# In the last image, q, k and the MLP's first layer use the two PSUM banks of the scan's gates

## The chip, the cores and the metric

The kernel runs on one core of one Trainium2 chip. The core has five instruction streams that run side by side and meet at semaphores: PE (matrix multiply; the profile shows its weight loads apart, as PEld), DVE (vector), ACT (scalar activation functions), POOL (general vector work) and SP, which here issues DMA transfers. Matmul results land in PSUM, which the program cuts into eight tiles of 128 partitions by 512 fp32 numbers; such a tile is called a bank below. The metric is the device time of one execution, in microseconds (us).

## The reference

Two layers work on a batch of 8 images of 192 channels by 64x64 pixels, in fp32.

Layer 0 widens to 384 channels with a 1x1 convolution, applies a 3x3 depthwise convolution, and forms gates from a 16-channel projection. In four directions it scans each chunk of eight columns:

```python
hn = l * x + gl * h_up + gm * h + gr * h_dn      # gl, gm, gr normalized by |gl| + |gm| + |gr| + eps
```

The four scans are weighted and added, normalized over channels, scaled by a global response norm (which needs sums over the whole image), and projected back to 192 channels.

Layer 1 is window attention on 8x8 windows with six heads, and an MLP:

```python
shortcut = _layer_norm(xs, norm1_g, norm1_b)
qkv = (xin @ qkv_w.T + qkv_b)                                     # 64 tokens per window
attn = einsum(_l2n(q), _l2n(k)) * temperature
attn = where(attn >= 16th largest of the row, attn, -100)
out = softmax(attn + rpb) @ v  ->  proj
x2 = shortcut + out
hdn = gelu(_layer_norm(x2) @ fc1_w.T + fc1_b) @ fc2_w.T + fc2_b   # 192 -> 768 -> 192
return x2 + hdn
```

## The kernel before

The kernel handles one image as three generators of steps: `front` (widening and convolution), `scan` (the gated scan, which ends in a per-image scale `sc`, `bb`), and `windows`, which runs `window_row` for each of the eight rows of windows. A row of windows is 8 image lines, 512 tokens, four tiles of 128 tokens. The front of image b+1, the scan of image b and the window rows of image b-1 are written down side by side. The window rows of the last image (b = 7) need the whole scan of that image, and no other scan follows; they run alone at the end.

Inside `window_row` the steps are, by line: load `zg` (L1032) and scale it (L1037); project tokens in two steps (L1052) with the first layer norm (L1059 to L1085); transpose the result into `sT` (L1017, L1025); project q and k, one step per tile of 128 tokens, each with its own PSUM tile `pq` (L1097, L1102), which ACT reads twice, once to copy it to `qk` (L1110) and once to square it (L1118); project the values (L1141, L1153); normalize q and k (L1162 to L1176) and transpose them (L1189, L1197); scores (L1217, L1231); top 16, mask, softmax (L1244 to L1298); transpose the attention (L1312, L1320); attend (L1332, L1345); project and add (L1366, L1378); second layer norm (L1389 to L1421); transpose to `xT` (L1434 to L1441); the MLP's first layer in three steps, each of which writes a pair of PSUM tiles `ph` (L1448, L1453, L1457) that ACT evacuates with the bias (L1464); GELU over all 768 hidden channels (L1473), then the activation table is set back (L1474); second layer plus residual (L1487), evacuation (L1501) and store.

PSUM is split into two pools. `n_ps` has two tiles under the tag `nb`; only `tile_of` of the scan uses it, for one of its gates (L678, `nb`). `l_ps` has six tiles under the tag `lp`; everything that calls `bank()` shares them, all the scan's other matmuls and all of `window_row`. One row of windows takes 34 tiles from it: 2 for tokens, 2 for `sT`, 4 `pq`, 2 for values, 4 to transpose q and k, 3 scores, 3 to transpose the attention, 2 to attend, 2 projections, 2 for `xT`, 6 `ph`, 2 for the second layer.

Nothing is issued while the generators run. `Held` is a tile that will be made later, and each `plan(engine, cost, fn, r=, w=)` records a step with what it reads and writes. `Plan.order` then schedules all steps of all eight images: a list scheduler that keeps a clock for every engine, models how long each step holds its engine (`act(n)`, `mm(slots, n)`, `dma(n)` = 350 ns of issue per transfer plus 2600 to landing, GELU 5400) and gives a step its PSUM tile only when one of its tag is free in the model. A step that makes two tiles starts when both are free. Within one tag and one `plan.lane`, steps that make tiles start in the order in which they were written; `window_row` changes the lane from stage to stage (`sT`, q, k and values are lane 7, the MLP lane 10), and the scan (lane 0) is kept a tile when it is ready for one. Among steps that can start without delay, the lowest `rank` goes first. `order` makes twelve rounds (`RUNS`): the first with ranks from the place in the program, each later one with due times from the round before, and keeps the round whose modelled length is shortest. The steps are then issued in that order on every engine. Each engine works through its stream in order, so a step that waits holds up all behind it on that engine.

The buffers in SBUF that set the distance between rows are `zg`, `qk`, `at`, `x2`, `xn` and `hd` with one copy, and `s0` and `v` with two.

Of the kernel before, what the change touches and what calls it, by code (L numbers as in the profile page):

```python
# [31 lines left out]
P = 128  # L32
B, DM, H, W = 8, 192, 64, 64
# [255 lines left out]
def tile_ss2d_then_window_attention(ctx: ExitStack, tc: tile.TileContext, a: dict, out: bass.AP):  # L289
# [164 lines left out]
    n_ps = ctx.enter_context(tc.tile_pool(name="n_ps", bufs=2, space=PSUM))  # L454
# [13 lines left out]
    log_c = {}  # L468
    log_half = blank("log_half", [P, 1], math.log(0.5) / 3)

    def bank(name="lp"):
        return Held(l_ps, [P, 512], name, tag="lp")

    def rsqrt(v, key, shape, name, gain=1.0):
# [20 lines left out]
    def front(b, xs, xsT):  # L495
# [14 lines left out]
        def project(ct, s):  # L510

            own = padded[ct * P : (ct + 1) * P]
            cols = slice(ct * P, (ct + 1) * P)
            pins = [bank() for _ in range(2)]

            def products():
# [27 lines left out]
        def convolve(ct, s):  # L544

            own = padded[ct * P : (ct + 1) * P]
            pc = bank()
            for k in range(2):
                strip = strips[k]
# [63 lines left out]
    def scan(b, xs, xsT, z, made):  # L613
# [14 lines left out]
        def proxy(t):  # L628

            x0 = Held(spool, [P, CT, 512], "x0", bufs=1)  # L630
            plan("SP", dma(), lambda: nc.sync.dma_start(x0(), xs()[:, :, t, :]), r=[xs], w=[x0])
            px = bank()

            def products():
# [374 lines left out]
    def window_row(b, g, z, sc, bb):  # L1009
# [84 lines left out]
        qk = Held(lpool, [P, NT, DIN], "qk", bufs=1)  # L1094
        nn = Held(small, [P, NT, 12], "nn")
        for tt in range(NT):
            pq = bank()  # L1097

            def projected(tt=tt, pq=pq):
                tok = slice(tt * P, (tt + 1) * P)  # L1100
                for ci in range(2):
                    nc.tensor.matmul(  # L1102
                        pq()[:, 0:DIN], lhsT=sT[:, ci, tok], rhs=w_qk[:, ci, :], start=ci == 0, stop=ci == 1
                    )

            plan("PE", mm(2, DIN), projected, r=["sT"], w=[pq, (qk, "room")])
            plan(
                "ACT",
                act(DIN),
                lambda tt=tt, pq=pq: nc.scalar.copy(qk()[:, tt, :], pq()[:, 0:DIN]),  # L1110
                r=[pq],
                w=[(qk, tt)],
            )
            sq = Held(lpool, [P, DIN], "sq", bufs=1)
            plan(
                "ACT",
                act(DIN),
                lambda pq=pq, sq=sq: nc.scalar.activation(sq(), pq()[:, 0:DIN], AF.Square),  # L1118
                r=[pq],
                w=[sq],  # L1120
            )
            plan(
                "DVE",
                vec(DIN),
                lambda tt=tt, sq=sq: nc.vector.tensor_reduce(
                    nn()[:, tt, :], sq().rearrange("p (h d) -> p h d", d=HD), AX.X, ALU.add
                ),
                r=[sq],
                w=[(nn, tt)],
            )  # L1130
            yield
# [313 lines left out]

        hd = Held(lpool, [P, NM, GT], "hd", bufs=1)
        for m2 in range(NM // 2):
            ph = [bank() for _ in range(2)]  # L1448

            def widened(m2=m2, ph=ph):  # L1450
                for k in range(2):
                    cols = slice((2 * m2 + k) * P, (2 * m2 + k + 1) * P)
                    nc.tensor.matmul(ph[k](), lhsT=w_f1[:, 0, cols], rhs=xT[:, 0, :], start=True, stop=False)  # L1453
                for k in range(2):
                    cols = slice((2 * m2 + k) * P, (2 * m2 + k + 1) * P)
                    own = slice(64 * k, 64 * k + 64)
                    nc.tensor.matmul(ph[k](), lhsT=w_f1[own, 1, cols], rhs=xT[own, 1, :], start=False, stop=True)  # L1457

            plan("PE", mm(3, GT), widened, r=["xT"], w=ph + [(hd, "room")])
            for k in range(2):  # L1460
                plan(
                    "ACT",
                    act(600),
                    lambda m=2 * m2 + k, p=ph[k]: nc.scalar.activation(  # L1464
                        hd()[:, m, :], p(), AF.Identity, bias=b_f1[:, m : m + 1]
                    ),
                    r=[ph[k]],
                    w=[(hd, 2 * m2 + k)],
                )
            yield  # L1470
# [51 lines left out]
    def windows(b, z, made):  # L1522
        for g in range(NG):
            yield from window_row(b, g, z, *made[b])
# [107 lines left out]
```

## Time and profile before

| what | us |
|---|---|
| median of 3 runs | 8295.51 (8274.17 to 8303.1) |
| the profiled execution's own time | 8293.82 |
| its span, first to last instruction | 8292.0 |
| PE / DVE / ACT / POOL busy in the span | 6951.0 / 6381.9 / 5488.0 / 5859.7 |
| last closing square of the last scan on ACT (L933) | 7782 |
| busy from 7860 to 8240: PE / ACT / DVE / POOL | 315.24 / 311.23 / 195.40 / 71.88 |

The span is the stretch that the trace covers; the profiled execution took 1.8 us more. A busy share is an average over stages: over the whole span the four engines are all between 66% and 84%, while after 7790 us DVE and POOL are mostly idle. "Idle before, releaser" names what ended an engine's wait. In the chain each step is followed back to what released it, so a wait that stands there delayed the end of the kernel. A matmul of fp32 numbers appears as two matmul instructions in the counts.

### The profile page before, as it was taken

The page shows a single profiled execution, that of the slowest core. Times are in us where ns is not written, and L with a number is a line of the kernel's source. Part 1 is how long each engine was busy: PE and PEld are TensorE (multiplying, and loading weights), DVE is VectorE, ACT ScalarE, POOL GpSimd, SP SyncE. Part 2 cuts the span into 40 slices and gives each one's busy share as a digit, 9 for nine tenths or more (in the row PEclk, how much of TensorE's full clock was granted, in tenths as well). Part 3 has the DMA queues.
Part 4 walks back from the last instruction along what each step waited for, and adds up shares of the span by engine and source line. Part 5 has one row for each costly group of instructions (what it writes and reads, how often), then busy time and mean ns, then how long its engine had stood idle before and what let it go on. Part 6 is the DMA issues. An engine that isn't in the chain of part 4 may idle for free.

```text
span 8292.0 us, 147108 instructions
## 1 busy us (share of the span) xinstructions
PE 6951.0 (84%) x51224; PEld 3600.7 (43%) x51224; DVE 6381.9 (77%) x15421; ACT 5488.0 (66%) x12537; POOL 5859.7 (71%) x5918
## 2 busy tenths in 40 slices
PE   5677688788988898888988898888888789888887
PEld 2333344444444444444444444444444444444454
DVE  1366777888788987888788887888888888888643
ACT  1355346766677666777577766777677676677787
POOL 0377877788778877788778777778788788877411
PEclk8887579788898788888898889888788887778898
DMA  6776146111542135411532126311111112111110
GB/s 175 193 191 180 42 128 165 50 44 45 139 129 74 52 96 138 107 45 56 157 103 77 46 76 171 91 46 46 57 41 50 43 41 66 41 48 41 30 22 15
DMA packets 1037948, 695.70 MB, mean 84 GB/s; under 512 B 704115, under 2 KB 860214, under 8 KB 1037206
## 3 DMA queue, kind: packets, MB, share of 16 engines
q1 hardware_dynamic: 1035830, 684.99, 30.9%
q8 instruction: 407, 6.67, 0.3%
q14 instruction: 335, 2.74, 0.1%
q10 hardware_dynamic: 1376, 1.30, 0.1%
HBM read 453.43 MB, written 232.67 MB: 83 GB/s over the span
## 4 chain that ended last, share of the span: by engine, by line
PE 23%; ACT 15%; DVE 14%; POOL 9%; DMA 5%; issue 4%; SPq 0%; POOLq 0%; DVEq 0%; ACTq 0%
PE g L678 6%; PE lp L1487 3%; PE lp L1453 2%; ACT at L1286 2%; ACT at L1298 2%; DMA zg<-z 2%; POOL pr L796 2%; PE lp L1052 2%; PE lp L565 2%; DVE pr L742 1%; PE lp L1102 1%; POOL pr L781 1%; ACT ab L735 1%; DMA strip<-pad 1%; POOL ab L766 1%
## 5 line engine op out<-in xcount | busy, mean ns | idle before, releaser
L678 PE MATMUL g<-xe,w_g 32*128 32x512 f32 x3648 | 1281.3, 777 | 284.0 <-DVE dx L833 90.3
L678 PE MATMUL g<-xo,w_g 32*128 32x512 f32 x3648 | 1218.2, 767 | 270.1 <-DVE dx L833 154.0
L796 POOL TENSOR_TENSOR pr<-pr,rr 128x512 f32<-128x512 f32 x672 | 872.5, 1298 | 369.4 <-ACT rr L779 320.5
L781 POOL TENSOR_TENSOR pr<-pr 128x512 f32<-128x512 f32 x672 | 887.2, 1321 | 339.7 <-DVE pr L742 254.8
L766 POOL TENSOR_TENSOR ab<-ab 128x512 f32<-128x512 f32 x672 | 873.4, 1300 | 269.6 <-ACT ab L735 264.7
L735 ACT ACTIVATE ab<-g 128x512 f32<-128x512 f32 x1344 | 778.7, 594 | 295.1 <-PE nb L678 175.5
L847 POOL TENSOR_TENSOR dx<-dx,hu 128x512 f32<-128x512 f32 x576 | 738.8, 1294 | 257.6 <-DVE hu L838 250.8
L565 PE MATMUL lp<-strip,w_cv 128*32 128x256 f32 x9216 | 678.3, 438 | 289.0 <-DMA strip<-pad 265.9
L785 POOL TENSOR_TENSOR pr<-pr 128x512 f32<-128x512 f32 x672 | 884.2, 1316 | 20.6
L678 PEld LDWEIGHTS g<-xe,w_g 32*128 32x128 f32 x3648 | 451.9, 219 | 835.0 <-DVE dx L833 206.5
L678 PEld LDWEIGHTS g<-xo,w_g 32*128 32x128 f32 x3648 | 423.4, 217 | 812.4 <-DVE dx L833 278.4
L777 ACT ACTIVATE rr<-nb,eps 128x512 f32<-128x512 f32 x672 | 460.4, 685 | 436.5 <-DVE nb L774 320.8
L1487 PE MATMUL lp<-hd,w_f 128*64 128x256 f32 (+1 forms) x2304 | 610.1, 505 | 63.4 <-ACT hd L1473 39.7
L792 DVE SCALAR_TENSOR_TENSOR nb<-nb,rr 128x512 f32<-128x512 f32 x672 | 464.7, 692 | 237.6 <-ACT rr L779 236.1
L565 PEld LDWEIGHTS lp<-strip,w_cv 128*32 128x32 f32 x9216 | 313.5, 122 | 659.3 <-issue 388.6
L855 POOL TENSOR_TENSOR y<-y,dx 128x512 f32<-128x512 f32 x384 | 593.9, 1555 | 1.8
L800 DVE SCALAR_TENSOR_TENSOR nb<-nb,pr 128x512 f32<-128x512 f32 x672 | 464.4, 691 | 152.5 <-POOL pr L796 148.1
L774 DVE TENSOR_TENSOR nb<-nb,ab 128x512 f32<-128x512 f32 x672 | 464.7, 691 | 128.9 <-POOL ab L766 98.8
L845 POOL TENSOR_TENSOR y<-hu,dx 128x512 f32<-128x512 f32 x192 | 247.3, 1296 | 418.8 <-DVE hu L838 415.7
L757 ACT ACTIVATE nb<-nb 128x512 f32<-128x512 f32 x672 | 397.8, 592 | 206.5 <-DVE pr L742 107.8
L838 DVE TENSOR_TENSOR hu<-g,hid 128x512 f32<-128x512 f32 x768 | 511.4, 678 | 4.6 <-PE g L678 1.7
L678 PE MATMUL nb<-xe,w_g 32*128 32x512 f32 x672 | 506.4, 844 | 8.8 <-DVE hid L807 8.6
(202 smaller groups left out, 17104.4 us busy)
## 6 DMA issues: line engine op xcount, KB each, us to landing
strip<-pad SPq DMA_DIRECT2D x1152, 132.0 KB
xd<-xsT SPq DMA_DIRECT2D x384, 256.0 KB
pad<-xin SPq DMA_DIRECT2D x192, 264.0 KB
xs<-st SPq DMA_DIRECT2D x192, 256.0 KB
xsT<-sn SPq DMA_DIRECT2D x192, 256.0 KB
xd<-xs SPq DMA_DIRECT2D x192, 256.0 KB
x<-xs SPq DMA_DIRECT2D x64, 768.0 KB
z<-y SPq DMA_DIRECT2D x64, 768.0 KB
```

The lines of the kernel that those rows point to most:

```text
L565: nc.tensor.matmul(pc()[q * RG : (q + 1) * RG, k * 256 : (k + 1) * 256].rearrange("p (h w) -> p h w", h=4), lhsT=w_cv[:, ct, q, dx, :], rh ...
L678: nc.tensor.matmul(dst, lhsT=w[rows, col : col + P], rhs=xp[rows, :], start=True, stop=True)
L735: lambda r=r: nc.scalar.activation(ab()[:, r, :], g[r](), AF.Abs),
L766: plan("POOL", gp(512), lambda: nc.gpsimd.tensor_add(ab()[:, 0, :], ab()[:, 0, :], ab()[:, 1, :]), w=[ab])
L774: plan("DVE", vec(512), lambda: nc.vector.tensor_add(nb(), nb(), ab()[:, 0, :]), r=[ab], w=[nb])
L781: plan("POOL", gp(512), lambda: nc.gpsimd.tensor_add(one(), one(), pr()[:, 1, :]), r=[(pr, 1)], w=[(pr, 0)])
L785: lambda: nc.gpsimd.tensor_add(one(), one(), pr()[:, 2, :]),
L796: plan("POOL", gp(512), lambda: nc.gpsimd.tensor_mul(one(), one(), rr()), r=[rr], w=[(pr, 0)])
L838: lambda: nc.vector.tensor_mul(like(hu(), d), like(pu(), d), state(d, ct)),
L847: plan("POOL", gp(512), lambda: nc.gpsimd.tensor_add(dx(), dx(), hu()), r=[hu], w=[dx])
L855: nc.gpsimd.tensor_add(y, y, dx().rearrange("p (c i) -> p i c", c=CH))
L1487: nc.tensor.matmul(dst[:, at : at + rhs.shape[-1]], lhsT=lhsT, rhs=rhs, **flags)
```

## The change

`bank` gets an argument `last`. With it, the tile comes from `n_ps` under the tag `nb` and not from `l_ps`. Two places pass it, and only for the last image: the four `pq` of each row and the three pairs `ph`. In the other seven images nothing is written differently. Matmuls, evacuations, costs and lanes are the same. In the last image ten of a row's 34 tiles come from the two `nb` tiles, and 24 from the six `lp` tiles. The planner sees the tags, so the order that it writes can differ too.

```diff
-    def bank(name="lp"):
+    def bank(name="lp", last=False):
+        if last:
+            return Held(n_ps, [P, 512], "nb")
         return Held(l_ps, [P, 512], name, tag="lp")
...
         for tt in range(NT):
-            pq = bank()
+            pq = bank(last=b == B - 1)
...
         for m2 in range(NM // 2):
-            ph = [bank() for _ in range(2)]
+            ph = [bank(last=b == B - 1) for _ in range(2)]
```

## The prediction

> **What bounds the kernel now.** The page comes first. Its engine line says that no engine is full over the span; its slices say where to look, because the change names the last image alone.
>
> ```profile
> PE 6951.0 (84%) x51224; PEld 3600.7 (43%) x51224; DVE 6381.9 (77%) x15421; ACT 5488.0 (66%) x12537; POOL 5859.7 (71%) x5918
> ...
> PE   5677688788988898888988898888888789888887
> ...
> DVE  1366777888788987888788887888888888888643
> ...
> POOL 0377877788778877788778777778788788877411
> ```
>
> DVE and POOL fall away in the last two to three slices of 207 us: the scan is over there and only window rows run. The last scan's closing square on ACT stands at 7782 us in the chain, so the stretch that the change can touch directly is the 510 us from there to 8292. The table by windows gives its steady part and its drain:
>
> ```profile
> 7860.00:8240.00 380.00, 315.24 (x2915) 199.62 (x2905) 195.40 (x981) 311.23 (x870) 71.88 (x201) 0.90 0.08 18
> ...
> 8240.00:8292.00 52.00, 35.49 (x260) 19.78 (x258) 2.93 (x10) 21.19 (x37) 1.94 (x10) 0.88 0.06 16
> ```
>
> The columns after the length are busy PE, PEld, DVE, ACT and POOL, then the clock and DMA. PE is busy 315 of 380 us and ACT 311, so PE and ACT bound the tail together: 65 us of PE idle time is all that any better order could win there. The scores of successive rows start at 7950.5, 8004.9, 8057.7 and 8107.2 us, about 52 us apart. The list of PE's waits in the same stretch says what ends that idle time:
>
> ```profile
> PE lp L1487 <- ACT hd L1473: 19.0, 3, 6.8
> ...
> PE lp L1312 <- ACT ot L1501: 4.6, 2, 2.3
> ...
> PE lp L1312 <- ACT qk L1110: 2.1, 3, 0.7
> ```
>
> The last two are waits for a bank: L1312 transposes `at`, and neither L1501 nor L1110 writes `at`; each frees a bank. They are 6.7 us together. The large one is data: the second layer waits for GELU.
>
> The chain, through one row, shows whose delay reaches the next row:
>
> ```profile
> 8015.97 0.02 issue
> 8016.00 2.22 ACT zg L1037 x3
> 8018.22 0.09 ACT ss_q L485
> 8018.31 1.15 ACT hd L1464 x2
> ...
> 8020.65 3.22 PE lp L1453 x4
> 8023.87 1.11 PE lp L1457 x4
> 8024.98 1.25 ACT hd L1464 x2
> ...
> 8028.01 2.76 ACT hd L1473
> ```
>
> The third pair of the MLP's first layer (L1453, L1457), its evacuation (L1464) and GELU (L1473) lie on it; GELU and evacuation are there in all eight rows of the last image.
>
> **How the banks are used now.** From the timelines of PE, ACT and DVE I took, for every PSUM tile from 7860 to 8240 us, its life from the first matmul that writes it to the end of its last reader. All six banks are taken at once for 32 us of the 380. The tiles that the change moves are alive for 335 bank-us (q, k: 28 tiles at 12.0) and 269 (first layer: 42 tiles at 6.4), 604 in all, and for 116 us there are three or more of them. After the change they have two banks, 760 bank-us: 79% used if no life gets shorter. The rest, 583 bank-us, has six banks, 2280: 26%. So the change relieves a pool that is full 8% of the time, and squeezes the tiles that held three banks or more 31% of the time.
>
> **The change part by part.** No instruction is added or removed and no DMA; the same matmuls, evacuations and stores run on the same engines. What changes is which bank a tile waits for, and through the planner the order on each queue (on SP that of the `zg` loads and the stores, on POOL that of the small norms; neither gets more to do). The sum is against the profiled execution, 8293.8 us (span 8292.0 and 1.8 around it), which stands 1.7 us under the median of 8295.5.
>
> First layer. Each of the three steps of a row takes two banks at once and writes both. Now the next pair finds other banks free: pairs start at 8261.51, 8264.95 and 8267.92, back to back. With two banks, pair n+1 can start only when both evacuations of pair n are done. Starting from the end of the first pair's evacuation as the profile has it, two more pairs follow, each 3.05 us of PE, 1.30 of evacuation and 0.10 of hand-over: 8.9 us to the end of the third evacuation. Row by row, first evacuation's end plus 8.9 against the third's end now: 7914.4 and 7919.8 give +3.5; 7965.1 and 7970.0, +4.0; 8019.5 and 8026.2, +2.2; 8073.1 and 8077.8, +4.2; 8121.8 and 8126.7, +4.0; 8171.1 and 8176.8, +3.2; 8223.2 and 8227.9, +4.2; 8266.3 and 8272.3, +2.9. That is 28.2 us by which GELU starts later over eight rows. The last two rows have next to nothing else to run, so their 7.1 count in full. In the other six (21.1) ACT has eight to sixteen exponentials (1.9 to 3.9 us) behind GELU that a new order can put ahead of it, which covers part; but the pair also waits where ACT itself stands in front of the `zg` transfer (2.63 us at 8016.0), since L1464 is queued behind L1037. I take three quarters, 15.8. Sum 22.9; bounds 2.9 (the last row alone) and 28.2. What is queued on PE behind a waiting pair is the next row's transposes (L1017) and its q and k (L1102); on ACT, behind the late evacuation, GELU and the shares.
>
> q and k. In four rows (7920, 8026, 8078, 8177 us) all four projections, 4.78 us of PE, run while ACT is in GELU, so that the second layer then starts without idle time; their banks are freed only 10.3 us after the matmuls, on average. With two banks, two projections (2.4 us) lose that place. The nearest cover is the two value projections (3.0 us), which read the same `sT` and keep their place among six banks. If it is used, the cost is nothing: the late pair takes the values' old place. If it is not, PE idles 2.4 us per row; and the second layer's first half, 5.31 us at 8031.4 where PE came without a gap, took 7.71 at 8233.9 after 6.82 idle, another 2.4. Bounds 0 and 19.2 (4.8 x 4). I take 2.4 x 4 = 9.6: the first pair's squares and copies (4 x 0.47 = 1.9) must also be pulled ahead of exponentials that are on the chain.
>
> Relief. The 6.7 us of L1312's bank waits can go; the ceiling is the 32 us in which six banks were taken. I take 6.7, because those are the waits that PE showed. What is late next there is `at` itself: at 8044.4 the transposes of the third part need the shares that end at 8043.2, so one of those waits shrinks to about half, and I don't count more.
>
> Sum: 8293.8 + 22.9 + 9.6 - 6.7 = 8319.6, about 8320, 0.3% over the median. The bounds by these terms alone: 8293.8 + 2.9 + 0 - 32 = 8265 and 8293.8 + 28.2 + 19.2 - 0 = 8341.
>
> **A page against the rows.** The Trainium skill, "Perfetto Trace Analysis", section "Matmul Optimizations", asks that all eight PSUM banks be used. By that alone, the sum would hold only the relief, 8287. The same page, section "Matmuls", asks that independent matmul groups rotate through different banks so that one's evacuation overlaps the next one's matmuls; that speaks against this change, since the first layer's pairs do so at 8264.95 and 8267.92 and no longer could. I go by the rows: six banks were full for 32 us, and the pairs' overlap is on the chain.
>
> **The rivals.** (1) Relief decides: faster. With q and k out of the six banks, tokens, transposes and attention run further ahead of ACT. For it: 65 us of PE idle and 69 of ACT idle in 380 us, and six full banks around 8038 to 8044, with PE's longest stops just after. Against it: two banks at 79%. It decides once running ahead wins more per row than the 3.2 us that the terms above cost it ((22.9 + 9.6 - 6.7) / 8); at 5 us per row it is 8293.8 - 8 x 1.8 = 8279; at the 32 us ceiling without any squeeze 8262.
>
> (2) Another order for the whole kernel. The planner makes twelve rounds and keeps the one that is shortest by its own costs. The last image changes each round's length, so another round may win, and then all eight images run in another order. The timeline gives the size that order can have: an image's closing mean (the first matmul of L986) stands at 1181.5, 2158.1, 3070.9, 4019.4, 4962.9, 5928.7, 6880.3 and 7797.9, periods of 913 to 977 us with a spread of 22. Seven such, independent, make 22 x 2.65 = 58 us either way: 8236 to 8352, about even, since nothing says that the round kept now is the best on the chip.
>
> (3) Hidden: the planner sorts evacuations ahead and both pairs fit into time in which PE had other work. For it: the two banks need only 3 x 4.45 for the first layer and 2 x (2.4 + 1.9) for q and k, about 22 us, of a 52 us row if evacuated promptly. Against it: ACT is 82% busy and the pairs' evacuation now ends 3.3 us after their matmuls on average. 8294 to 8300.
>
> **How the numbers follow.** A measurement of this kernel tells about 0.3%, 25 us, from no change: 8271 and 8320 are the limits. The squeeze outweighs the relief: 0.54, 8304 to 8345; its centre lies on the upper limit, and I put 0.38 over it and 0.16 under it, since each unsorted wait adds and the `zg` transfer took 6.00 us at 8010 where the planner counts 2.95. Relief decides: 0.16, of it 0.12 faster. Another order: 0.24, of it 0.10 faster, 0.03 the same, 0.11 slower. Hidden: 0.06, the same. So faster 0.22, same 0.29, slower 0.49. The range leaves out the outer part of the second rival on both sides: 8256 to 8368.
>
> **What would show it.** Right: up to about 7500 us the two traces agree in order and times; pairs of L1453 stand apart by over 4.3 us in each row, with L1464 of the pair before as releaser; in the last row the third evacuation ends 2.9 us later after the first pair's start; L1312 no longer waits for L1501 or L1110; rows are 54 to 56 us apart. Wrong: L986 of the first images at other times (rival 2); rows under 51 us apart (rival 1); pairs apart but GELU as soon after the row's scores as now (rival 3). What would make it wrong above all is that the planner fills the gaps between pairs with the values and transposes that the six banks now let run.

## The result, and the profile after

The changed kernel takes 8323.65 us in the median (8322.48 to 8348.03, five runs), the kernel before 8294.23 us. The ratio over all executions is 1.0049 with a 95% interval of 1.0031 to 1.0066; the two medians alone give 1.0035. That is slower, as forecast, and under 4 us from the predicted 8320. The number is nearer than its working deserves, as the traces show.

PE's streams of the two kernels are the same for the first 47852 of 51224 matmul instructions, up to 7831 us in the trace after, shortly after the last scan has ended. The planner keeps its eleventh round in both. (By its own count, which is no time of the chip, the kept round grew from 7660.3 to 7701.1 us.) So both traces can be cut at an instruction that stands in both, the closing mean of the last image: L986 before, L988 after, where two lines were added. What lies behind that cut is the tail; it holds the eight rows of the last image and the end of the last row of the image before. In the table by windows, first of the kernel before and then of the kernel after, the columns behind the length are busy PE, PEld, DVE, ACT and POOL, then the clock:

```profile
7797.90:8292.00 494.10, 405.81 (x3620) 254.33 (x3618) 208.74 (x1018) 376.13 (x1009) 80.14 (x242) 0.90 0.09 20
```

```profile
7805.50:8346.30 540.80, 426.94 (x3620) 261.85 (x3618) 206.63 (x1018) 379.88 (x1009) 81.30 (x242) 0.87 0.08 19
```

The tail went from 494.1 to 540.7 us to the last instruction's start, 46.6 us more. The same 3620 matmul instructions held PE 21.1 us longer, at a granted clock of 0.87 for 0.90; PE's idle time rose from 88.3 to 113.9 us, 25.6 more. ACT did the same work in 3.8 us more. So the added time, as PE spends it, is waiting and running slower, about half and half. As ACT spends it, nearly all of it is waiting, so this split says where PE's time went and not yet why.

What PE waited for in the tail, before:

```profile
PE lp L1487 <- ACT hd L1473: 27.5, 5, 6.8
PE lp L1017 <- ACT s L1085: 9.0, 5, 2.7
PE lp L1434 <- ACT xn L1421: 7.8, 3, 3.3
PE lp L1312 <- ACT ot L1501: 4.6, 2, 2.3
...
PE lp L1312 <- issue: 4.3, 2, 3.2
...
PE lp L1189 <- DVE qk L1176: 2.1, 3, 1.5
```

and after:

```profile
PE lp L1489 <- ACT hd L1475: 19.0, 5, 5.4
PE lp L1436 <- ACT xn L1423: 18.9, 6, 6.1
PE lp L1314 <- issue: 15.8, 6, 5.2
PE nb L1455 <- ACT hd L1466: 14.3, 10, 4.1
PE lp L1191 <- DVE qk L1178: 7.2, 5, 2.5
...
PE nb L1104 <- ACT sq L1120: 4.9, 3, 2.3
...
PE nb L1104 <- ACT hd L1466: 2.5, 3, 2.1
PE lp L1314 <- ACT ot L1503: 2.3, 1, 2.3
```

Three lines are waits at the two banks: L1455 and L1104 waiting for ACT to release a tile, 21.7 us together. The waits for the second layer norm (`xn`) and for the normalized `qk` grew by 16.2 us, and those are no bank waits. The wait for GELU shrank by 8.5. The line "issue" at L1314, where the profile names no releaser, grew by 11.5; in ACT's timeline each of its six waits ends 0.1 us after a share of the softmax (L1300), which writes the `at` that L1314 reads, so it too looks like a wait for data and not for a bank.

In PE's timeline of the last row the pairs stand apart:

```profile
8312.41 2.97 PE L1455 MATMUL nb<-xT,w_f 128*128 128x512 f32 x4
8315.31 1.13 PE L1459 MATMUL nb<-xT,w_f 64*128 64x512 f32 x4
8317.21 1.98 PE L1455 MATMUL nb<-xT,w_f 128*128 128x512 f32 x4 [0.77 <-ACT hd L1466]
8319.12 1.13 PE L1459 MATMUL nb<-xT,w_f 64*128 64x512 f32 x4
8321.02 1.98 PE L1455 MATMUL nb<-xT,w_f 128*128 128x512 f32 x4 [0.77 <-ACT hd L1466]
```

In this row the pairs started 3.4 and 3.0 us apart before and start 4.8 and 3.8 us apart now (the first L1455 still takes 2.97 us, the next ones 1.98). The next pair starts 0.77 us after the end of the pair before, at 8317.21, when ACT has released one of the two tiles (its first evacuation ends at 8317.16, the second at 8317.74); it doesn't wait for both.

### The profile page after: what moved, and what is told of

Same layout as the page of the kernel before. It is cut to its first block, busy times and chain, and to the rows that moved or that the text cites. A ratio compares the mean times of both kernels' runs of the same rounds, so it can differ in the third digit from the quotient of the medians.

```text
span 8346.3 us, 147122 instructions
## 1 busy us (share of the span) xinstructions
PE 6985.1 (84%) x51224; PEld 3616.4 (43%) x51224; DVE 6375.7 (76%) x15421; ACT 5495.5 (66%) x12537; POOL 5864.9 (70%) x5918
## 4 chain that ended last, share of the span: by engine, by line
PE 24%; ACT 15%; DVE 14%; POOL 8%; DMA 5%; issue 4%; SPq 0%; POOLq 0%; DVEq 0%; ACTq 0%
PE g L680 6%; PE lp L1489 3%; ACT at L1288 2%; ACT at L1300 2%; DMA zg<-z 2%; PE lp L567 2%; PE lp L1054 2%; POOL pr L798 2%; PE lp L1455 2%; DVE pr L744 1%; ACT ab L737 1%; DMA strip<-pad 1%; POOL pr L783 1%; DVE nb L802 1%; DVE dx L835 1%
```

## The experiments

The body ahead of the cut scatters: in thirteen traces whose streams there are the same, L986 or its counterpart starts between 7774.5 and 7805.5 us. The tail didn't where that could be seen: two traces of the changed kernel both gave 540.7. So each experiment below has its ratio, and its tail behind the cut in one trace; the tail tells the small differences apart. The medians agree with the tails to about 10 us in each experiment, but not in the change's first measurement (29.4 for 46.6), so a difference of less than that between two rows rests on single traces. (Line numbers are those of each experiment's own kernel, up to four higher than before.)

| kernel | tail, us | against before | ratio, 95% interval |
|---|---|---|---|
| before | 494.1 | | |
| the change | 540.7, 540.7 | +46.6 | 1.0049 (1.0031 to 1.0066); 1.0060 (1.0036 to 1.0084) |
| first layer alone | 537.2 | +43.1 | 1.0047 (1.0035 to 1.0059) |
| q, k alone | 538.3 | +44.2 | 1.0046 (1.0033 to 1.0058) |
| half of each | 507.0 | +12.9 | 1.0013 (1.0003 to 1.0022) |
| values alone | 530.9 | +36.8 | 1.0039 (1.0026 to 1.0051) |
| first layer, streams of before | 523.8 | +29.7 | 1.0032 (1.0020 to 1.0043) |
| first layer's streams, six banks | 527.5 | +33.4 | 1.0047 (1.0031 to 1.0063) |
| the change's streams, six banks | 531.5 | +37.4 | 1.0034 (1.0022 to 1.0047) |
| values' streams, six banks | 538.5 | +44.4 | 1.0050 (1.0035 to 1.0065) |
| tokens, attention, second layer | 494.1 | 0.0 | 1.0006 (0.9995 to 1.0017) |
| `zg` cost as measured | 485.8 | -8.3 | 0.9998 (0.9987 to 1.0010) |

### One part at a time

First theory, the prediction's: squeeze. Two banks hold ten of a row's tiles, so pairs and projections wait for evacuations. Rival: the values. Before, they stood behind q and k in one queue for a bank (tag `lp`, lane 7); with q and k under another tag they may go first.

The first layer alone, without the edit at `pq`:

```diff
-            pq = bank(last=b == B - 1)
+            pq = bank()
```

> Only the first layer's pairs take the two gate banks in the last image; q and k stay with the six. Squeeze (each pair must wait for the evacuation of the pair before): most of the change's cost is here, as the prediction had it (22.9 of 32.5 us before relief), so 10 to 25 us slower than before, and pairs of L1455 stand over 3.5 us apart. Order of the values (the change's cost comes from the values' projection, which no longer queues behind q and k for a bank): nothing here, within 5 us of before. Relief: faster than before by up to 7 us.

q and k alone, without the edit at `ph`:

```diff
-            ph = [bank(last=b == B - 1) for _ in range(2)]
+            ph = [bank() for _ in range(2)]
```

> Only q and k take the two gate banks in the last image; the first layer stays with the six. Squeeze: the smaller part, 5 to 15 us slower than before (9.6 predicted). Order of the values: the whole cost of the change is here, 25 to 35 us slower. If both parts have a cost of their own and it adds up, the first layer alone and this one sum to the change's 29 us; if each alone costs about as much as both, they share one limit.

Half of each:

```diff
-            pq = bank(last=b == B - 1)
+            pq = bank(last=b == B - 1 and tt % 2 == 1)
...
-            ph = [bank(last=b == B - 1) for _ in range(2)]
+            ph = [bank(last=b == B - 1 and k == 0) for k in range(2)]
```

> In the last image the first tile of each pair of the first layer and every second q-k tile take the gate banks, the others stay with the six: five of a row's 34 tiles in the two banks, and a pair can start before the pair ahead of it is fully evacuated. Squeeze: the cost goes, within 8 us of before, and the relief of 5 to 7 us may show. If any use of the gate banks in the last image costs (another placement in PSUM, another order): 15 to 30 us slower, as with the change.

The values alone, against the kernel before with `bank`'s new argument:

```diff
-            pv = bank()
+            pv = bank(last=b == B - 1)
```

> Only the two tiles of the values take the gate banks in the last image; q, k and the first layer stay with the six. Their life is 3.4 us and there are two, so nothing is squeezed. Squeeze: within 5 us of before. Order of the values (they may now start ahead of q and k, for which the next row's scores wait): 15 to 35 us slower than before, with L1143 ahead of L1104 on PE and the rows' scores 2 to 4 us further apart.

The ratios are 1.0047, 1.0046, 1.0013 and 1.0039. Each part alone costs nearly as much as both together (43.1 and 44.2 against 46.6 us), so there is no sum of two costs. The values alone cost 36.8 us, though they can't squeeze anything: two tiles a row, alive for 3.4 us. The squeeze gives no account of that. As a wait on the chip it gives none of q and k alone either, where the profile names no wait of PE for one of the two banks: the only waits of L1104 in that tail are for its input `sT`, and what stands high are waits ahead of the transposes of `at` (L1314):

```profile
PE lp L1314 <- issue: 26.8, 8, 5.2
...
PE lp L1314 <- POOL at L1273: 17.4, 4, 4.3
...
PE nb L1104 <- ACT sT L1027: 1.3, 2, 0.7
```

The values' order, in turn, gives no account of the first layer alone, where the values stayed with q and k. PE's timeline of values alone has the order that the rival expected, the values between the projections of q and k:

```profile
7843.02 1.56 PE L1104 MATMUL lp<-w_qk,sT 128*128 128x384 f32 x4
7844.41 1.46 PE L1143 MATMUL nb<-w_v,sT 128*128 128x192 f32 x8
7845.71 1.45 PE L1104 MATMUL lp<-w_qk,sT 128*128 128x384 f32 x4
7847.00 1.46 PE L1143 MATMUL nb<-w_v,sT 128*128 128x192 f32 x8
```

In the same row before, all of L1102 came first:

```profile
7862.24 5.76 PE L1102 MATMUL lp<-w_qk,sT 128*128 128x384 f32 x16 [0.55 <-ACT sT L1025]
7867.83 2.76 PE L1141 MATMUL lp<-w_v,sT 128*128 128x192 f32 x16
```

Half of each shows that using the banks isn't what costs: five tiles a row lie there, and the tail is 12.9 us longer, not 46.6. That is still more than the 8 us I allowed it; its streams differ from those of before too. In it PE waited only 2.0 us longer and was busy 11.0 longer with the same instructions (416.8 for 405.8, at a clock of 0.89 for 0.90).

### Banks without order, order without banks

The new theory: what costs is the order that the planner writes when it sees two banks. (For the values alone, where nothing is squeezed, the planner's own count is 34.5 us above that of the kernel before.) Its rival remains the waits at the banks. They come apart if the planner counts one pool and the tile is made in the other. Banks without order, for the first layer:

```diff
     def bank(name="lp", last=False):
+        h = Held(l_ps, [P, 512], name, tag="lp")
         if last:
-            return Held(n_ps, [P, 512], "nb")
-        return Held(l_ps, [P, 512], name, tag="lp")
+            h.args = n_ps, [P, 512], F32, "nb", "nb", n_ps.bufs
+        return h
```

> The first layer's pairs lie in the two gate banks in the last image, but every engine's stream is that of the kernel before: the planner still counts the pairs among the six. Waits at the banks (pairs really wait for each other's evacuation, and that is the cost): at least the 28.2 us that the prediction worked out row by row for just this case, so 20 to 35 us slower than before, with waits of L1455 for L1466 on PE. Order (the cost is in the streams that the planner writes when it sees two banks): under 10 us slower, because ACT runs the exponentials in the time in which GELU is late, and only the drain's 3 to 7 us remain.

Order without banks, for the first layer alone, the whole change and the values alone:

```diff
         if last:
-            return Held(n_ps, [P, 512], "nb")
+            h = Held(n_ps, [P, 512], "nb")
+            h.args = l_ps, [P, 512], F32, name, "lp", l_ps.bufs
+            return h
```

> The streams of the kernel in which the first layer alone has the gate banks, but all of the last image's tiles lie in the six banks as before. Waits at the banks: the cost goes, within 10 us of before. Order: 35 to 45 us slower, like first_layer_alone, with the same row whose scores come 92 us after those of the row before.

> The streams of the changed kernel, but q, k and the first layer lie in the six banks as before and the gate banks stay empty. Waits at the banks: within 10 us of before. Order: 30 to 45 us slower than before, as the change.

> The streams of values_alone, but the values lie in the six banks as before. The order explains that kernel, which has nothing to squeeze: 25 to 40 us slower than before. If instead the two gate banks themselves are slow to use in the last image, it is within 10 us of before.

With the old streams and the banks moved, the tail is 29.7 us longer (ratio 1.0032). PE's waits in it name the pairs:

```profile
PE nb L1456 <- ACT hd L1467: 31.6, 17, 5.1
PE lp L1490 <- ACT hd L1476: 25.0, 5, 6.7
```

Against what I expected of the order, nothing was hidden: waits at the banks alone are a real cost when nothing is moved around them. With the new streams and the six banks, where the gate banks stay empty, the tails are 33.4, 37.4 and 44.4 us longer (1.0047, 1.0034, 1.0050). So the order alone costs as much too. Both theories hold in part. If the streams stay, PE pays at the banks; if the planner knows of the two banks, it writes streams that avoid part of those waits (14.3 us for L1455 in the change where 31.6 stood) and are slower for other reasons. For the whole change, 37.4 of the 46.6 us come with the streams alone, and the two banks add 9.2. Such shares depend on what is changed first: for the first layer the banks cost 29.7 us in the old streams and 9.7 in the new ones (43.1 less 33.4).

What the slower streams wait for, in the change's order on six banks:

```profile
PE lp L1491 <- ACT hd L1477: 21.0, 6, 5.4
PE lp L1438 <- ACT xn L1425: 18.8, 6, 6.1
PE lp L1316 <- ACT at L1302: 17.4, 6, 5.3
PE lp L1021 <- ACT s L1089: 13.9, 5, 6.3
PE lp L1491 <- ACT ot L1505: 6.0, 1, 6.0
...
PE lp L1491 <- ACT oT L1349: 3.6, 1, 3.6
```

The first four are waits within one row's own chain (GELU, second norm, softmax, first norm); the stream has no work of the neighbouring row in that place. The last two are waits for one of the six banks, since L1491 reads neither `ot` nor `oT`: these streams were written for ten tiles a row less in the six, so part of the 37.4 us is bank waiting after all, at the six banks and not at the two. The distances between the scores of successive rows show where the tail gets longer: 42, 49, 54, 53, 50, 58 and 43 us before, and 40, 55, 60, 64, 44, 62 and 51 here. In the first layer's order one pair of rows is 88 us apart and the next 42. Which single displacement starts it isn't settled. For q and k the banks without the order were not tried: in three of the eight rows of the old streams ACT squares the third tile before it copies the first, and the third would need the first one's bank, so PE and ACT would wait for each other. But the trace of q and k alone, with its new streams, shows the 44.2 us without a wait at the two banks.

### The change again

> The changed kernel once more, for a second trace of its tail. The tail counted from the last image's L988 to the end was 540.7 us against 494.1 before. Order and waits in the tail: 530 to 550 us again, and 35 to 47 us over the kernel before in the median. If the first trace was a long execution and the true cost is the 28 us that the predicted waits alone explain: about 522 us.

The kernel is `after` without an edit: 8323.94 us, ratio 1.0060 (1.0036 to 1.0084), tail 540.7 us. 46.6 us are 0.56%, inside both intervals. PE was busy for 427.3 us in the tail at a clock of 0.87, as in the first trace (426.9), so the slower matmuls repeat with the order. The first trace was a long execution (8348 us), but not because of its tail. This second one (8343 us) is the longest of its four, too; no short execution of the change was traced.

### Relief without squeeze

In the last image the tokens, the attention's output and the second layer take the two banks, and nothing else does:

```diff
-            pz = bank()
+            pz = bank(last=b == B - 1)
...
-        po = [bank() for _ in range(2)]
+        po = [bank(last=b == B - 1) for _ in range(2)]
...
-            pf = bank()
+            pf = bank(last=b == B - 1)
```

> In the last image tokens, attention output and the MLP's second layer take the two gate banks (six of a row's 34 tiles); q, k, values and the first layer stay with the six. Nothing long-lived is squeezed and the streams are nearly those of before. The predicted relief: 5 to 7 us faster than before, with no wait of L1314 for L1503 on PE. No worth in relief (the bank was not what those transposes waited for last): within 3 us of before.

1.0006 (0.9995 to 1.0017) and a tail of 494.1 us, the same as before to a tenth. L1314 no longer waits for L1503, but it does for the next bank to come free:

```profile
PE lp L1314 <- ACT qk L1112: 6.5, 3, 2.6
```

Before, the two waits were 4.6 and 2.1, 6.7 together. The wait has moved to the release of q and k (L1112 writes no `at`), and nothing was won.

### The order on its own

If streams are worth 30 us for the worse, perhaps also for the better. In the tail ACT waits for the `zg` transfer, which the planner counts too short. Banks as before, in the last image alone:

```diff
-        plan("SP", dma(), lambda: nc.sync.dma_start(zg(), z()[...]), r=[z], w=[zg])
+        plan("SP", (350.0, 5650.0 if b == B - 1 else 2600.0), lambda: nc.sync.dma_start(zg(), z()[...]), r=[z], w=[zg])
```

> The kernel before, banks untouched; in the last image the planner counts 5.65 us from the issue of the zg load to its landing and not 2.6. If the order in the tail is worth tens of us either way, as the order-alone runs say, an order without ACT standing 2 to 2.6 us in front of zg in five rows is 8 to 20 us faster than before. If only the bank moves make order matter: within 5 us.

ACT's waits for `zg`, 14.0 us in six places of the tail before, are gone. The tail is 8.3 us shorter, at the low end of what was expected, and the ratio, 0.9998 (0.9987 to 1.0010), can't tell that from nothing. With more rounds of the planner:

```diff
-    RUNS = 12
+    RUNS = 24
```

> As zg_cost_as_measured, with 24 planning rounds for 12. The planner then keeps its nineteenth round, with another order for all eight images, which it counts 27 us shorter than the kernel before. If its count carries over to the chip as it did in the tail: 15 to 35 us faster than before. If over whole images its count says little: anywhere within 40 us either way.

1.0016 (1.0006 to 1.0026), slower. The planner counted this order, which differs in all images, 27 us shorter. So its count, which came near most of the tails where the body stood still (40.8 us for the change's 46.6, none for the relief's 0.0, but 0.1 for the 12.9 of half of each), doesn't carry over to another order of the whole.

## Why the prediction was right or wrong

**Direction, and the number.** Slower was right, and moving the tiles to the two banks was the reason, though mostly through the order that the planner then wrote. That the number came out close is luck: the sum put 25.8 us on the change where the tail shows 46.6, and the medians of five executions happened to be 29.4 us apart. In the second measurement they were 50.1 apart.

**First layer, 22.9 us.** With the old streams this step was right at its upper end, and its discount was wrong. The prediction had GELU later by 3.5, 4.0, 2.2, 4.2, 4.0, 3.2, 4.2 and 2.9 us from row to row, 28.2 in all; measured from the cut, with the streams kept, the growth was 3.8, 4.5, 2.0, 3.5, 4.9, 0.9, 6.6 and 2.5, 28.7 in all, and the tail grew by 29.7. The three quarters for six rows took off 5.3 that nothing hid. The make-up was off: a pair starts when the first tile is free, so the last pitch in the drain is 3.8 us where the working had 4.45, and of the 29.7 us PE was busy for 10.1 with the same instructions (415.9 for 405.8), which the step didn't have. That the total fits is partly luck.

**q and k, 9.6 us.** Too small, and not a term that can be added. Alone the part costs 44.2 us, with the other 46.6. The lack of a free bank that it priced isn't what PE waits for: alone, q and k show no wait at the two banks. The cover that I named, the values in the place of the late projections, is what the planner did, and I had called its cost nothing. In the runs of the values, whose order has it too, the tail is 36.8 us longer, on six banks 44.4; that this one move is the cause isn't shown, since the rest of the tail was ordered anew with it.

**Relief, 6.7 us.** Zero, where it was tried without the squeeze: the wait moved to the next bank that comes free. In the change itself 2.3 us of it are left (L1314 waiting for L1503).

**The step that failed** is adding three terms on fixed streams and counting the planner's new order only as cover. 37.4 of the 46.6 us stand in streams that need no moved bank. Slower matmuls were in the sum for q and k only; in the tail they are 21.1 of the 46.7 us between the two windows. The 108 instructions of the first layer's L1453 took 637 ns each before and, as L1455, 682 after (691 for the 96 in the gate banks). For the same reason PE's 65 us of idle time were not all that an order can win or lose: PE's busy time for the tail's 3620 instructions lies between 403.1 and 427.3 us in the runs of the table.

**The page.** The Trainium skill, "Perfetto Trace Analysis", section "Matmul Optimizations", asks for all eight banks. This case doesn't show a gain from it: the tail with six tiles a row in the idle two has the length of the one without. The rows had pointed that way, with all six banks taken for 32 of 380 us.

**Rivals.** Relief (1) didn't decide. Another order for the whole kernel (2) didn't come; it came within the last image, where I had not priced it. Hidden (3): no row of this case shows it.

**The signs.** L1453's pairs do stand apart, 13 of the 16 distances by over 4.3 us as said and three by 3.8, and ahead of L1455 PE waited ten times for L1464's counterpart. The last row's third evacuation ends 2.2 us later after its first pair's start, where I had said 2.9. L1312's counterpart still waits 2.3 us for L1501's, where I had said no wait. Rows are 54 us apart on average (65 to 445 us from the cut over seven distances) for 50 before, as said. I had said that the two traces would agree in times up to 7500 us; their streams do, their times differ by up to 8.6 us at the closing means (4019.4 and 4010.8).

## What to carry to other kernels

Where a scheduler writes the order, moving a buffer to another pool is also a new order: take the two apart by counting one pool and allocating from the other before pricing either. Here two unused banks won nothing, because the wait for a bank that went only made way for the next; move a short-lived tile there first and see whether the wait goes or only changes its releaser. When two kernels share their streams up to a point, cut both traces at an instruction there: here the tail repeated to a tenth of a microsecond, where whole executions scattered by tens.

## What was not expected of the hardware

The tail of 540.7 us came out the same in two executions whose bodies ended 5.5 us apart (7805.5 and 7800.0), and 494.1 in two kernels with nearly the same streams; in these traces the scatter lies ahead of the last image's tail, and no run here says from what. And the same matmuls don't cost the same in another order: with the change 25.6 us more idle time on PE came with 21.1 us more busy time, at a clock of 0.87 for 0.90. There is no fixed price between the two: with the old streams on the moved banks it was 19.7 us idle and 10.1 busy, with half of each 2.0 idle and 11.0 busy (clock 0.89 in both). Which waits slow the matmuls isn't shown.
